# Second attention of a graph-network kernel: exponentials straight from PSUM, a shift from the first columns, one-input looks, a shorter epilogue, the reciprocal root as a power on GpSimd

## Chip, core and metric

One core of one Trainium2 chip. The metric is the device time of one execution in microseconds (us). The repeats of one kernel differ by under 0.4%. In profile lines PE is the engine that multiplies matrices (TensorE), DVE is VectorE, ACT ScalarE and POOL GpSimd; L12 is line 12 of the kernel that was run, so line numbers differ between kernels.

## The reference, cut to what matters

Four graph layers on 3327 nodes with 256 features. The change concerns the last one, which runs two steps of an attention whose rows keep only their largest probabilities, up to 90% of the mass:

```python
for n in range(STEPS):                       # 2 steps; the change is in the second
    q, k = Xa @ W1.T @ W2.T, Xa @ W3.T
    probs = softmax(q @ k.T)                 # 3327 x 3327
    A = probs * (smallest set of largest entries with sum >= 0.9)
    A = A / A.sum(-1)
    Xf = R @ Xf                              # diffusion, R = normalized (adj + I)
    Xa = A @ Xa
    Z = Z + Xf @ U1[n].T + Xa @ U2[n].T
h = layernorm(X + Z) * g + b
return layernorm(X + h)
```

## The kernel before: the parts concerned

Rows are worked in 26 tiles of 128. A tile ("a row" from here on) is searched one ahead: `ahead(it + 1)` makes the logits of the next row and searches them while `step(it)` attends, diffuses and finishes this one. The text is not the order of execution: the framework fixes the order of each engine's instructions at compile time, and the place in the text is only one of the things that decide it.

```python
# logits(): eight pieces of 416 columns, each copied out of PSUM
for c0 in range(0, half, KC):
    for a in (0, DA):
        nc.tensor.matmul(pl[:, :w], q[a:a + DA, :], kT[a:a + DA, c0:c0 + w], start=True, stop=True)
        nc.scalar.copy(e[:, c:c + w], pl[:, :w])

def search_long(work, e, total, v, kept):
    nc.vector.max(m8, e)                               # needs the whole row
    nc.vector.tensor_scalar(hneg, m8[:, 0:1], -0.5, LN15 / 2, ...)
    nc.scalar.activation(junk, e, AF.Exp, bias=hneg, scale=0.5, accum_out=root)
    exponentials(e, m8[:, 0:1], total)                 # e = exp(e - max), total = its sum
    c1 = 0.301 * (total / root) ** 2                   # first threshold
    nc.scalar.activation(junk, e, AF.Sign, bias=c1, scale=-1.0, accum_out=sg)   # count
    over(c1, m1)                                       # "look": mass of e >= c1, two inputs
    ...                                                # c2 by small steps
    over(c2, m2)
    ...                                                # c3
    nc.vector.scalar_tensor_tensor(z, e, c3, e, is_lt, mult, accum_out=rest)
    top = ranked(work, segment_tops(work, z), RPT)     # 32 MAX8 of 104 columns, 7 rounds
    ...
    for k in range(0, TIES, 8):                        # two full-width replaces
        nc.vector.match_replace(z, rep[:, k:k + 8], z if k else e, 2.0)
    nc.vector.scalar_tensor_tensor(e, z, v, e, is_gt, mult, accum_out=kept)   # "last product"

es = [ahead(0)]
for it in range(nt):
    if it + 1 < nt:
        es.append(ahead(it + 1))
    step(it, ...)                                      # attention, diffuse, finish
```

## Time and profile before

| | us |
|---|---|
| time, median of 4 | 5088.1 (5085.5 to 5091.3) |
| one row of the second attention | 54.06 |
| of it DVE works / stands still | 46.4 / 7.7 |
| PE works / ACT works | 40.6 / 23.1 |

A row is the mean distance between the starts of the masking product into `z` in successive rows; work is the busy time of an engine in windows of whole rows, and standstill is the rest. The groups, windows, waits and chain stand in the prediction below. This is the timeline of ACT in one row of the kernel before (start us, us, line, what):

```profile
4726.40 1.28 ACT L70 ACT_TABLE_LOAD   x1
4727.70 0.29 ACT L70 ACTIVATE std<-mv,eps_t 128x1 f32<-128x1 f32 x1
4728.01 1.28 ACT L439 ACT_TABLE_LOAD   x1
4729.31 3.07 ACT L439 ACTIVATE e<-e,neg 128x3328 f32<-128x3328 f32 x1
```

Between the two exponentials of this row ACT loads a table for the root, takes a root of one column, and loads the exponentials' table again, while DVE waits for the second exponential: two loads of 1.28 us. This is the worst place; in the whole stage 7 loads stand in front of the full-scale exponential (L439) as here, and 24 in front of the half-scale one (L474).

### The profile page before, as it was taken

Reading aid. Unit: us, or ns where it says so; the run is one execution under the profiler, and the core shown is the slowest. Engines: PE = TensorE matmul, PEld = TensorE weight load, DVE = VectorE, ACT = ScalarE, POOL = GpSimd, SP = SyncE. Lnnn points to the kernel's source line nnn. Section 1 sums busy time; section 2 is a strip of 40 time slices with the busy share of each in tenths; the row PEclk is TensorE's granted clock in tenths of the full one; section 3 lists DMA queues with packets and bytes.
Section 4 is the critical chain, followed back from the end, with each engine's and each line's share of the span. In section 5 each row is a group of like instructions: output and inputs, shape, how many; then the busy total and the mean of one; then the engine's idle time right before and its main releaser. Section 6 shows DMA issues by size and latency. Waiting matters only on the chain. (4 is left out here: it accounts for less than half of the span.)

```text
span 5089.8 us, 44369 instructions
## 1 busy us (share of the span) xinstructions
PE 4067.5 (80%) x16218; PEld 2926.3 (57%) x16218; DVE 3402.9 (67%) x6846; ACT 1790.1 (35%) x2868; POOL 5.5 (0%) x58
## 2 busy tenths in 40 slices
PE   8999986677767776779978999999577778787686
PEld 7878862222322223567756777777366556565565
DVE  1111129798797988799944544453388888888886
ACT  0001124334343243355533333333333443443442
POOL 0000000000000000000000000000000000000000
PEclk9999987777777777889978999999588888888888
DMA  5433320000000000122211111111001001011010
GB/s 176 137 127 132 131 74 0 0 0 0 0 0 0 0 0 0 58 94 105 102 35 35 47 54 54 50 45 54 1 29 43 30 30 43 29 36 38 30 34 27
DMA packets 59325, 239.76 MB, mean 47 GB/s; under 512 B 7105, under 2 KB 21568, under 8 KB 55632
## 3 DMA queue, kind: packets, MB, share of 16 engines
q1 hardware_dynamic: 59088, 236.74, 14.0%
q8 instruction: 132, 2.16, 0.2%
q14 instruction: 105, 0.86, 0.1%
HBM read 233.31 MB, written 3.41 MB: 47 GB/s over the span
## 5 line engine op out<-in xcount | busy, mean ns | idle before, releaser
L105 PE MATMUL acc<-X,at 128*128 128x256 f32 x2704 | 611.4, 381 | 11.9 <-DMA at<-in_adjT 11.9
L271 PE MATMUL y<-db,ident 128*128 128x512 f32 (+1 forms) x896 | 501.0, 715 | 138.6 <-DVE db L269 138.4
L105 PEld LDWEIGHTS acc<-X,at 128*128 128x128 f32 x2704 | 508.5, 191 | 77.4 <-issue 12.3
L265 DVE TENSOR_TENSOR_SCAN h<-dA,carry,db 128x512 f32<-128x512 f32 (+1 forms) x448 | 504.3, 1188 | 2.2
L253 PE MATMUL ps<-dbc,ident 48*128 48x512 f32 (+1 forms) x448 | 294.1, 783 | 226.6 <-ACT row L256 226.6
L271 PEld LDWEIGHTS y<-db,ident 128*128 128x128 f32 x896 | 207.7, 244 | 453.3 <-DVE db L269 239.4
L118 ACT COPY wt<-ps 128x512 f32<-128x512 f32 (+1 forms) x546 | 278.6, 555 | 448.2 <-PE ps L116 444.4
L116 PE MATMUL ps<-ident,e 128*128 128x128 f32 x1352 | 204.7, 301 | 252.7 <-DVE e L545 215.7
L260 ACT ACTIVATE dA<-dt,A_log 128x512 f32<-128x512 f32 (+1 forms) x448 | 273.0, 680 | 371.8 <-DVE h L265 371.7
L120 PE MATMUL acc<-Xa,wt 128*128 128x256 f32 x1352 | 340.0, 407 | 15.5 <-ACT wt L118 14.5
L116 PEld LDWEIGHTS ps<-ident,e 128*128 128x128 f32 x1352 | 176.6, 156 | 297.5 <-issue 270.2
L120 PE MATMUL acc<-H,wt 128*128 128x256 f32 x1352 | 313.9, 386 | 29.0 <-ACT wt L118 26.4
L120 PE MATMUL acc<-X,wt 128*128 128x256 f32 x1352 | 310.2, 383 | 21.5 <-ACT wt L118 19.3
L253 PEld LDWEIGHTS ps<-dbc,ident 48*128 48x128 f32 x448 | 96.6, 242 | 392.7 <-ACT row L256 276.7
L94 ACT COPY xt<-ps 128x256 f32<-128x256 f32 x234 | 82.5, 374 | 651.9 <-PE ps L92 629.5
L120 PEld LDWEIGHTS acc<-Xa,wt 128*128 128x128 f32 x1352 | 272.7, 206 | 66.8 <-ACT wt L118 27.1
L105 PE MATMUL acc<-xa,at 128*128 128x257 f32 x1352 | 307.4, 381 | 0.0
L105 PE MATMUL acc<-Xf,at 128*128 128x256 f32 x1352 | 301.7, 379 | 0.0
L120 PEld LDWEIGHTS acc<-H,wt 128*128 128x128 f32 x1352 | 251.7, 191 | 76.8 <-ACT wt L118 44.7
L120 PEld LDWEIGHTS acc<-X,wt 128*128 128x128 f32 x1352 | 252.5, 190 | 70.3 <-ACT wt L118 38.2
L415 PE MATMUL ps<-kT,q 64*128 64x416 f32 x832 | 255.0, 615 | 36.8 <-ACT q L401 25.8
L105 PEld LDWEIGHTS acc<-xa,at 128*128 128x128 f32 x1352 | 255.2, 190 | 36.9 <-issue 0.7
(238 smaller groups left out, 6006.4 us busy)
## 6 DMA issues: line engine op xcount, KB each, us to landing
at<-in_adjT SPq DMA_DIRECT2D x104, 832.0 KB, 4.4
at<-in_adjT SPq DMA_DIRECT2D x104, 576.0 KB, 3.7
ad<-in_adj SPq DMA_DIRECT2D x26, 1663.5 KB, 6.8
at<-in_adjT SPq DMA_DIRECT2D x52, 512.0 KB, 3.5
xa<-in_x SPq DMA_DIRECT2D x1, 3328.0 KB, 12.7
xt<-in_xT SPq DMA_DIRECT2D x26, 128.0 KB, 4.0
out<-h SPq DMA_DIRECT2D x25, 128.0 KB, 1.7
w_in<-in_w_in SPq DMA_DIRECT2D x1, 1024.0 KB, 5.1
```

The costliest lines, as they stand in the source:

```text
L94: nc.scalar.copy(t, pt)
L105: nc.tensor.matmul(acc, at[:, j, :], rhs[:, j0 + j, :], start=(j0 + j == 0), stop=(j0 + j == nt - 1))
L116: nc.tensor.transpose(pt[:, j, :], w[:, (j0 + j) * P:(j0 + j + 1) * P], ident)
L118: nc.scalar.copy(wt[:, :m, :], pt[:, :m, :])
L120: nc.tensor.matmul(acc, wt[:, j, :], rhs[:, j0 + j, :], start=(j0 + j == 0), stop=(j0 + j == nt - 1))
L253: nc.tensor.matmul(ps[:, :w], ident[:R, r:r + 1].to_broadcast([R, P]), dbc[:, :w], start=True, stop=True)
L260: nc.scalar.activation(dA[:, g, :], dt[:, g, :], AF.Exp, scale=A[:, g, s:s + 1])
L265: nc.vector.tensor_tensor_scan(h[:, g, :], dA[:, g, :], db[:, g, :], initial=carry[:, s, g:g + 1], op0=ALU.mult, op1=ALU.add)
L271: nc.tensor.matmul(ys[g][:, :w], ident, db[:, g, :], start=(s == 0), stop=(s == DS - 1))
L415: nc.tensor.matmul(pl[:, :w], q[a:a + DA, :], kT[a:a + DA, c0:c0 + w], start=True, stop=True)
```

## The change

Its intent: DVE bounds the second attention, so take a full-width maximum and some small instructions off it, let the exponentials start as soon as pieces of logits arrive, and keep ACT in one table. The exponentials read the logits where PE leaves them (PSUM) instead of a copy. The shift is what is subtracted before the exponential: it was the maximum of the whole row and is now that of its first piece of 416 columns.

```diff
+            q = query(work, psum, xs, it)
+            for i in range(nk):                              # eight pieces
+                nc.tensor.matmul(pl, q[a:a + DA, :], kT[a:a + DA, c0:c0 + w], start=True, stop=True)
+                if neg is None:                              # first piece alone
+                    nc.vector.max(m8, pl)
+                    nc.vector.tensor_scalar_mul(neg, m8[:, 0:1], -1.0)
+                    nc.vector.tensor_scalar_mul(hneg, m8[:, 0:1], -0.5)
+                nc.scalar.activation(e[:, c:c + w], pl, AF.Exp, bias=neg, accum_out=totals[:, i:i + 1])
+                nc.scalar.activation(junk[:, :w], pl, AF.Exp, bias=hneg, scale=0.5, accum_out=roots[:, i:i + 1])
+            nc.vector.reduce_sum(total, totals, axis=AX.X)
+            nc.vector.reduce_sum(root, roots, axis=AX.X)
...
-                nc.vector.scalar_tensor_tensor(djunk, e, c, e, op0=ALU.is_ge, op1=ALU.mult, accum_out=m)
+                nc.vector.tensor_scalar(djunk, e, c, 0.0, op0=ALU.max, op1=ALU.add, accum_out=f)
+                nc.scalar.activation(ajunk, e, AF.Sign, bias=c, scale=-1.0, accum_out=sg)   # in both looks
+                nc.vector.tensor_scalar(k, sg, -0.5, npad / 2, op0=ALU.mult, op1=ALU.add)
+                nc.vector.tensor_scalar(m, k, -float(npad), c, op0=ALU.add, op1=ALU.mult)
+                nc.vector.tensor_add(m, m, f)
...
         def diffuse(...):
-            nc.vector.tensor_add(t, acc, xs[:, it, :])
-            nc.vector.tensor_scalar_mul(dst, t, rdeg[:, it:it + 1])
+            nc.gpsimd.tensor_scalar(t, xs[:, it, :], rdeg[:, it:it + 1], None, op0=ALU.mult)
+            nc.vector.scalar_tensor_tensor(dst, acc, rdeg[:, it:it + 1], t, op0=ALU.mult, op1=ALU.add)
...
         def finish(...):                                     # twice: variance -> rstd
+            nc.gpsimd.tensor_scalar(rs, mv[:, 1:2], EPS, None, op0=ALU.add)
+            nc.gpsimd.tensor_tensor(rs, rs, mhalf, op=ALU.pow)
-            layernorm(h, h)
-            nc.vector.tensor_mul(h, h, g3)
-            nc.vector.tensor_add(h, h, b3)
-            nc.vector.tensor_add(h, h, X[:, it, :])
-            layernorm(h, h)
+            nc.vector.scalar_tensor_tensor(h, h, mv[:, 0:1], g3, op0=ALU.subtract, op1=ALU.mult)
+            nc.vector.scalar_tensor_tensor(h, h, rs, xb, op0=ALU.mult, op1=ALU.add)
+            ...
+            nc.scalar.activation(h, h, AF.Identity, scale=rs, bias=nb)
```

More of the change, by code (lines that the diff above doesn't have):

```diff
@@ L34 @@
 UNDER = 24.0
+HUGE = 1e38
 KC = 416
@@ L365, in gnn_kernel @@
         nc.vector.memset(ones, 1.0)
+        mhalf = pool.tile([P, 1], F32, name="mhalf")
+        nc.vector.memset(mhalf, -0.5)
         count = pool.tile([P, TIES], F32, name="count")
@@ L454, in limit, with search_short @@
             return lim
-        def search_short(work, e, total, v, kept):
+        def search_short(work, psum, xs, kT, it, total, v, kept):
+            e = logits(work, psum, xs, kT, it, 3)
             top = ranked(work, segment_tops(work, e), RP0)
@@ L463, in search_short, with search_long, t1 @@
             nc.vector.scalar_tensor_tensor(e, e, v, e, op0=ALU.is_ge, op1=ALU.mult, accum_out=kept)
-        def search_long(work, e, total, v, kept):
-            m8 = sm.tile([P, 8], F32, name="m8")
-            nc.vector.max(m8, e)
-            hneg = sm.tile([P, 1], F32, name="hneg")
-            nc.vector.tensor_scalar(hneg, m8[:, 0:1], -0.5, LN15 / 2, op0=ALU.mult, op1=ALU.add)
-            junk = work.tile([P, npad], BF16, name="ajunk", bufs=1)
-            root = sm.tile([P, 1], F32, name="root")
-            nc.scalar.activation(junk, e, AF.Exp, bias=hneg, scale=0.5, accum_out=root)
-            exponentials(e, m8[:, 0:1], total)
+            return e
+        def search_long(work, psum, xs, kT, it, total, v, kept):
+            def t1(name, w=1):
+                return sm.tile([P, w], F32, name=name)
+            e = work.tile([P, npad], F32, name="e", bufs=3)
+            if npad > n:
+                nc.gpsimd.memset(e[:, n:], 0.0)
+            q = query(work, psum, xs, it)
+            neg, hneg = None, None
+            nk = half // KC * 2
+            roots, totals = t1("roots", nk), t1("totals", nk)
+            for i in range(nk):
+                a, c0 = (0, DA)[i % 2], i // 2 * KC
+                c = c0 + (half if a else 0)
+                w = min(KC, n - c)
+                pl = psum.tile([P, 512], F32, name="ps")[:, :w]
+                nc.tensor.matmul(pl, q[a:a + DA, :], kT[a:a + DA, c0:c0 + w], start=True, stop=True)
+                if neg is None:
+                    m8 = t1("m8", 8)
+                    nc.vector.max(m8, pl)
+                    neg, hneg = t1("neg"), t1("hneg")
+                    nc.vector.tensor_scalar_mul(neg, m8[:, 0:1], -1.0)
+                    nc.vector.tensor_scalar_mul(hneg, m8[:, 0:1], -0.5)
+                nc.scalar.activation(e[:, c:c + w], pl, AF.Exp, bias=neg, accum_out=totals[:, i:i + 1])
+                junk = work.tile([P, KC], BF16, name="rjunk")
+                nc.scalar.activation(junk[:, :w], pl, AF.Exp, bias=hneg, scale=0.5, accum_out=roots[:, i:i + 1])
+            root = t1("root")
+            nc.vector.reduce_sum(total, totals, axis=AX.X)
+            nc.vector.reduce_sum(root, roots, axis=AX.X)
             lim = limit(total)
-            def t1(name):
-                return sm.tile([P, 1], F32, name=name)
             c1 = t1("c1")
@@ L484, in search_long, with look @@
             nc.vector.scalar_tensor_tensor(c1, c1, 0.301, c1, op0=ALU.mult, op1=ALU.mult)
-            z = work.tile([P, npad], F32, name="z", bufs=1)
-            djunk = work.tile([P, npad], BF16, name="djunk", bufs=1)
-            def over(c, m):
-                nc.vector.scalar_tensor_tensor(djunk, e, c, e, op0=ALU.is_ge, op1=ALU.mult, accum_out=m)
-            m1, m2, sg = t1("m1"), t1("m2"), t1("sg")
-            nc.scalar.activation(junk, e, AF.Sign, bias=c1, scale=-1.0, accum_out=sg)
-            over(c1, m1)
-            rc = t1("rc")
+            def look(c, i):
+                f, sg, k, m = (t1(f"{x}{i}") for x in ("lf", "ls", "lk", "lm"))
+                djunk = work.tile([P, npad], BF16, name="djunk", bufs=1)
+                nc.vector.tensor_scalar(djunk, e, c, 0.0, op0=ALU.max, op1=ALU.add, accum_out=f)
+                ajunk = work.tile([P, npad], BF16, name="ajunk", bufs=1)
+                nc.scalar.activation(ajunk, e, AF.Sign, bias=c, scale=-1.0, accum_out=sg)
+                nc.vector.tensor_scalar(k, sg, -0.5, npad / 2, op0=ALU.mult, op1=ALU.add)
+                nc.vector.tensor_scalar(m, k, -float(npad), c, op0=ALU.add, op1=ALU.mult)
+                nc.vector.tensor_add(m, m, f)
+                return k, m
+            k1, m1 = look(c1, 1)
+            rc, na = t1("rc"), t1("na")
             nc.vector.reciprocal(rc, c1)
-            na, k1 = t1("na"), t1("k1")
             nc.vector.tensor_scalar(na, m1, lim, rc, op0=ALU.subtract, op1=ALU.mult)
-            nc.vector.tensor_scalar(k1, sg, -0.5, npad / 2, op0=ALU.mult, op1=ALU.add)
             den, nu, p, q = t1("den"), t1("nu"), t1("p"), t1("q")
@@ L512, in search_long @@
             nc.vector.tensor_sub(big, k1, na)
-            nc.vector.tensor_scalar(big, big, 32.0, 1e9, op0=ALU.is_lt, op1=ALU.mult)
-            over(c2, m2)
+            nc.vector.tensor_scalar(big, big, 32.0, HUGE, op0=ALU.is_lt, op1=ALU.mult)
+            k2, m2 = look(c2, 2)
             s, dm, lo, hi = t1("s"), t1("dm"), t1("lo"), t1("hi")
@@ L530, in search_long @@
             rest, base = t1("rest"), t1("base")
+            z = work.tile([P, npad], F32, name="z", bufs=1)
             nc.vector.scalar_tensor_tensor(z, e, c3, e, op0=ALU.is_lt, op1=ALU.mult, accum_out=rest)
@@ L535, in search_long @@
             cs = crossing(work, v, top, 8 * RPT, base, lim)
-            r, rep = t1("r"), sm.tile([P, TIES], F32, name="rep")
+            r, rep = t1("r"), t1("rep", TIES)
             nc.vector.tensor_sub(cs, cs, top)
@@ L540, in search_long @@
             nc.vector.scalar_tensor_tensor(cs, cs, lim, top, op0=ALU.is_lt, op1=ALU.mult, accum_out=r)
-            nc.vector.tensor_scalar(rep, count, r, -5.0, op0=ALU.is_ge, op1=ALU.mult)
+            nc.vector.tensor_scalar(rep, count, r, -HUGE, op0=ALU.is_ge, op1=ALU.mult)
             nc.vector.tensor_scalar_add(rep, rep, v)
             for k in range(0, TIES, 8):
-                nc.vector.match_replace(z, rep[:, k:k + 8], z if k else e, 2.0)
+                nc.vector.match_replace(z, rep[:, k:k + 8], z if k else e, HUGE)
             nc.vector.scalar_tensor_tensor(e, z, v, e, op0=ALU.is_gt, op1=ALU.mult, accum_out=kept)
+            return e
         def normalizer(kept, total):
@@ L619, in diffuse, with rstd @@
         def diffuse(work, atp, psum, dst, xs, it):
+            t = work.tile([P, D], F32, name="t")
+            nc.gpsimd.tensor_scalar(t, xs[:, it, :], rdeg[:, it:it + 1], None, op0=ALU.mult)
             acc = aggregate(atp, psum, it, xs, D, 9)
-            t = work.tile([P, D], F32, name="t")
-            nc.vector.tensor_add(t, acc, xs[:, it, :])
-            nc.vector.tensor_scalar_mul(dst, t, rdeg[:, it:it + 1])
+            nc.vector.scalar_tensor_tensor(dst, acc, rdeg[:, it:it + 1], t, op0=ALU.mult, op1=ALU.add)
+        def rstd(mv):
+            rs = sm.tile([P, 1], F32, name="rs3")
+            nc.gpsimd.tensor_scalar(rs, mv[:, 1:2], EPS, None, op0=ALU.add)
+            nc.gpsimd.tensor_tensor(rs, rs, mhalf, op=ALU.pow)
+            return rs
         def finish(work, psum, it, xf2, xa2):
+            xb = work.tile([P, D], F32, name="t")
+            nc.gpsimd.tensor_tensor(xb, X[:, it, :], b3, op=ALU.add)
             pz = psum.tile([P, D], F32, name="acc")
@@ L632, in finish @@
             nc.vector.tensor_add(h, pz, X[:, it, :])
-            layernorm(h, h)
-            nc.vector.tensor_mul(h, h, g3)
-            nc.vector.tensor_add(h, h, b3)
-            nc.vector.tensor_add(h, h, X[:, it, :])
-            layernorm(h, h)
+            mv = sm.tile([P, 2], F32, name="mv3")
+            stats(mv, h)
+            rs = rstd(mv)
+            nc.vector.scalar_tensor_tensor(h, h, mv[:, 0:1], g3, op0=ALU.subtract, op1=ALU.mult)
+            nc.vector.scalar_tensor_tensor(h, h, rs, xb, op0=ALU.mult, op1=ALU.add)
+            mv = sm.tile([P, 2], F32, name="mv3")
+            stats(mv, h)
+            rs = rstd(mv)
+            nb = sm.tile([P, 1], F32, name="nb")
+            nc.vector.scalar_tensor_tensor(nb, mv[:, 0:1], -1.0, rs, op0=ALU.mult, op1=ALU.mult)
+            nc.scalar.activation(h, h, AF.Identity, scale=rs, bias=nb)
             m = min(P, n - it * P)
@@ L674, in ahead @@
                 def ahead(it):
-                    e = logits(work, psum, xs, kT, it, 3)
-                    search(work, e, tot_all[:, it:it + 1], v_all[:, it:it + 1], kept_all[:, it:it + 1])
-                    return e
+                    return search(work, psum, xs, kT, it, tot_all[:, it:it + 1], v_all[:, it:it + 1], kept_all[:, it:it + 1])
                 es = [ahead(0)]
```

## The prediction

> **What bounds the kernel now**
>
> I read the page first (slices, costliest groups), then a table of windows over the last third, then the groups by form, the waits and the chain inside the second attention only. The slices show PE at 9 tenths nearly everywhere up to slice 28 and dropping to 5 to 8 after it, while DVE rises to 8: the last eleven or twelve slices are the second attention, and there the bound changes hands. It runs from about 3637 us (where DVE starts on its first row) to the end at 5089.8, so some 1453 us or 29% of the span. Almost all of the change lies in it; in the first attention only the small diffusion epilogue changes.
>
> Its 26 row tiles repeat in a pattern of three (three e buffers). The windows of three such patterns, columns as in their head line:
>
> ```profile
> core 0: us, PE busy (x) PEld busy (x) DVE busy (x) ACT busy (x) POOL busy (x), PEclk, DMA share, GB/s
> 3200.00:3300.00 100.00, 93.87 (x456) 75.04 (x455) 48.84 (x183) 35.37 (x66) 0.29 (x3) 1.00 0.16 52
> 4149.50:4312.25 162.75, 122.07 (x536) 97.31 (x535) 139.15 (x369) 69.19 (x101) 0.29 (x3) 0.85 0.11 34
> 4312.25:4473.90 161.65, 121.30 (x536) 96.11 (x535) 139.04 (x369) 69.28 (x101) 0.29 (x3) 0.86 0.11 35
> 4473.90:4636.60 162.70, 122.05 (x536) 97.24 (x535) 139.19 (x369) 69.18 (x101) 0.29 (x3) 0.85 0.11 34
> ```
>
> A row thus takes (162.75+161.65+162.70)/9 = 54.1 us; DVE works 46.4 of it (86%), PE 40.6, ACT 23.1. The first line is the first attention: there PE works 94% at clock 1.00. So in the second attention PE is not the limit; it waits, and its clock falls to 0.85. DVE stands still 7.7 us a row. What it waits for, over the whole stage:
>
> ```profile
> DVE lim L453 <- ACT e L439: 84.9, 25, 3.9
> DVE c L482 <- ACT ajunk L474: 56.8, 17, 4.5
> DVE t L622 <- PE acc L105: 26.7, 5, 23.9
> DVE h L632 <- PE acc L630: 16.0, 14, 3.5
> DVE rs L71 <- ACT std L70: 13.4, 11, 2.2
> ```
>
> The reader is to see that the two exponentials of a row cost DVE (84.9+56.8)/26 = 5.4 us of standstill a row, though ACT is not full: they cannot start before the row's maximum is known, and the maximum needs the whole copied row. The chain inside three rows says the same: DVE lines for the most part, and the two exponentials in between.
>
> ```profile
> by line: DVE djunk L489 13.7%; DVE z L544 11.9%; DVE cand L423 10.0%; issue 8.2%; DVE z L531 6.9%; DVE m L469 6.5%; ACT e L439 5.8%; DVE top L430 4.5%; DVE cand L432 4.1%; ACT ajunk L474 3.0%; DVE e L545 2.4%; PE acc L630 2.1%; ACT L474 1.6
> ```
>
> Durations that I use (last numbers before the bar are the mean ns of one):
>
> ```profile
> L489 DVE SCALAR_TENSOR_TENSOR djunk<-e,c 128x3328 bf16<-128x3328 f32 x52 | 191.6, 3684 | 1.8
> L469 DVE MAX8 m<-e 128x8 f32<-128x3328 f32 x26 | 93.7, 3602 | 72.1 <-ACT e L416 72.1
> L79 DVE TENSOR_SCALAR h<-h,mv,rs 128x256 f32<-128x256 f32 x52 | 21.3, 410 | 0.5
> L635 DVE TENSOR_TENSOR h<-h,ln_b 128x256 f32<-128x256 f32 x26 | 10.9, 419 | 0.1
> L623 DVE TENSOR_SCALAR xf<-t,rdeg 128x256 f32<-128x256 f32 x26 | 8.7, 335 | 0.0
> L498 DVE TENSOR_SCALAR na<-m,lim,rc 128x1 f32<-128x1 f32 x26 | 7.1, 272 | 0.0
> L439 ACT ACTIVATE e<-e,neg 128x3328 f32<-128x3328 f32 x26 | 79.8, 3069 | 0.4
> L474 ACT ACT_TABLE_LOAD x24 | 30.8, 1283 | 65.8 <-DVE hneg L471 55.9 <-DVE neg L438 9.7
> ```
>
> **What the Trainium skill says**
>
> "VectorE: DVE Perf Modes", section "The perf-mode tier table", gives an fp32 SBUF tensor_scalar two elements a cycle and a tensor_tensor one. The trace agrees: the standardize of 256 columns takes 410 ns where the same form on one column takes 272, so 138 ns for the columns, half of the 267 that the second form's 419 contains. That would make a one-input look of 3328 columns some 1.75 us shorter than the two-input one. But "SBUF — State Buffer", section "Who interferes with whom", excepts from the two-port modes the form of tensor_scalar that also writes out its accumulator, and the looks are that form. No instruction of the kernel before is of that form, so its trace cannot decide. I follow the page: no gain in rate.
>
> "ScalarE: Activation LUTs", section "What ACT_TABLE_LOAD costs", gives 1283 ns for a load (the trace: 1283) and about 280 ns + 0.833 ns a column for an activation with a pointer bias (3052 for 3328 columns; the trace: 3069). For 416 columns that is an estimate of 0.63 us. Its section "Table sets" puts exp and sqrt in different sets, which is why the trace has 63 loads in this stage (32 at the square root, 24 and 7 at the exponentials).
>
> "GPSIMD Engine Reference", section "Elementwise — side-by-side cycle accounting", has GpSimd about half as fast as DVE on two inputs; a 128x256 add would then be an estimated 0.8 us. GpSimd is empty here (under 0.1 us a row), so only its latency can matter. No trace shows a power there.
>
> **The change part by part, per row of the second attention**
>
> 1. *Row maximum.* Out: one MAX8 over 3328 columns, 3.60. In: one over 416 columns from PSUM; the slope is 3602/3328 = 1.08 ns, so about 0.55 with overhead. DVE -3.05.
> 2. *Looks.* Two two-input looks of 3.68 plus a 0.08 read become two one-input looks of, by the page, about 3.6 plus 0.08: -0.1 (at the double rate it would be -3.6). Each now needs a Sign count on ACT (the first had it). More small steps on the path: k, m, m for each look in place of one k in all, about +0.85, and two short sums of partial totals, +0.35.
> 3. *Epilogue.* Diffusion: 0.42+0.33 becomes one 0.42: -0.33. Finish: out are two reciprocals (0.31), two standardizes (0.82), three tensor_tensors (1.26); in are two scalar_tensor_tensors (0.84) and one small product (0.15): -1.4. Both also take 63 table loads (1.28 each, 3.1 us a row) off ACT.
>
> Sum on DVE: -3.05-0.1+0.85+0.35-0.33-1.4 = -3.7, so 46.4 becomes 42.7 us of work a row.
>
> 4. *Exponentials from PSUM.* Out on ACT: eight copies (about 0.43 to 0.5 each, 3.7), two exponentials and their reads (6.4), the loads (3.1), two roots (0.6): -13.8. In: 16 exponentials of 416 columns, each with an accumulator read. In the trace an exponential with its read advances ACT by 3.19 us for 3328 columns; 2912 columns less at 0.833 leave 0.76, so 16 x 0.76 = 12.2; a second Sign (3.2); a last scaling of 128x256 (0.47). +15.9. ACT goes from 23.1 to about 25 us a row, still half of the row.
>
> What matters more is when they run. The exponentials no longer wait for a complete row; they can run while DVE ranks and replaces in the row before (about 20 us of DVE work), so most of the 5.4 us standstill should go. But not all: the first maximum and its two sign changes stand somewhere in DVE's strict order behind a 3.6 us instruction or two, then 12.2 us of ACT follow, and the first constant of the search waits for the last sum. I leave 3.5 us of the 7.7 of standstill.
>
> Row: 42.7 + 3.5 = 46.2 us against 54.1, -7.9. Times 26: -205. Filling and draining change little: the first row saves a maximum and part of its two exponentials (about 5 us), the last finish perhaps 1. The first attention loses 0.33 us of DVE a row where DVE is half idle and PE works 94%: nothing.
>
> 5090 - 205 - 5 = 4880; I put it at 4890, since a schedule seldom gives all.
>
> **Rivals**
>
> *PE and ACT take over in the logits.* Today PE makes a row's eight pairs of logits in 4.5 us; each bank will now be held for two exponentials, 1.5 us, so the stage lasts 12.2 and PE, with three such banks, is held by ACT for 7 to 8 us. If PE ran attention (16.5), diffusion (11.2), finish (5.5), query (2) and logits (12.5) strictly in this order after each search, a row would be 47.7 us plus handing over, about 48.5, whatever DVE saves: -146, a time of 4945. For it: this is PE's order in two of the three rows of the pattern, and PE is in order. Against it: in the third row the diffusion's matmuls are already interleaved with the attention's, so the static order does fill PE's gaps with the next ready work. Denser work would also lift PE's clock from 0.86 towards the 1.00 of the first attention.
>
> *The looks run at the double rate.* Then DVE falls to 39 us, PE (40.6 busy, about 37 to 39 at clock 1.00) and DVE are level, and a row is 43 to 45: 4805 to 4855. For it: plain tensor_scalars do so in this trace. Against it: the page's exception.
>
> *Only the work goes and the standstill stays.* The wait for the exponentials moves from the long ones to the last of sixteen short ones, or the second Sign is late for the second look because ACT is at attention's copies. Then -3.7 x 26 = -96: 4994, within 2%.
>
> *GpSimd's small steps stretch the finish.* A variance goes DVE, GpSimd twice, DVE, twice a row. If each trip cost 2 us of standstill, 4 us a row would be lost. The roots' trips cost DVE 13.4/26 = 0.5 us a row before, with table loads, because other DVE work was put between; I expect the same.
>
> **Range and chances**
>
> The 8-in-10 range covers the double-rate looks at half their effect on one side (4825) and a PE and ACT bound row with some handing over on the other (4970). Faster by over 2% means under 4988, 3.9 us a row; the work removed from DVE alone is 3.7, so almost any gain of overlap suffices: 0.87. Within 2%: 0.11, if the standstill stays or a new one comes. Slower: 0.02, for an order in which PE, ACT and DVE wait for one another in turn.
>
> **What would show it right or wrong**
>
> Right: no full-width maximum and no table loads in the rows; looks of 3.6 to 3.7 us; DVE busy near 42.7 us a row and over 90% of it; the wait for the exponentials under 2 us a row; ACT near 25. A look near 2 us means the page's exception doesn't hold here. The PE bound shows as matmuls of the logits waiting for the exponentials by 5 us or more a row with DVE under 88%. A long wait of the normalizing steps for GpSimd shows the last rival. All this fails as a whole if rows before the last third change their length, or if the fallback search for unresolved rows runs, which would show as a new stretch of work after a pass.

## The result, and the profile after

| | before | after |
|---|---|---|
| time, median of 4 | 5088.1 | 5079.1 (5077.4 to 5079.8) |
| ratio after to before | | 0.9981, 95% interval 0.9964 to 0.9999 |
| one row of the second attention | 54.06 | 54.06 |
| DVE works / stands still, a row | 46.4 / 7.7 | 43.9 / 10.2 |
| ACT works, a row | 23.1 | 22.3 |

Ratios are the mean time of one kernel's fast runs over that of the other's in the same rounds, so not quite the ratio of the medians quoted. 4890 was predicted, within 4825 to 4970: wrong. The row did not get shorter at all. What was gained is from before the steady rows: in the profiled executions the third row's masking product starts at 3755.57 us against 3770.30, and from there on rows of both kernels take 54.0 to 54.1 us (at the end these two executions are 13.2 us apart, the medians 9.0).

A window of three rows of the changed kernel (columns as in its head line):

```profile
core 0: us, PE busy (x) PEld busy (x) DVE busy (x) ACT busy (x) POOL busy (x), PEclk, DMA share, GB/s
4314.24:4476.40 162.16, 126.25 (x537) 93.56 (x536) 131.61 (x376) 66.95 (x157) 9.91 (x21) 0.84 0.11 35
```

DVE's work fell from about 139 us in three rows to 131.61 (131.70 and 131.66 in the windows beside it), but the window of three rows is as long as before. What fills it is in the waits (us in total, times, longest):

```profile
PE ps L492 <- ACT rjunk L501: 248.3, 48, 10.1
ACT e L499 <- DVE neg L497: 240.3, 24, 10.5
DVE tot_all L503 <- ACT e L499: 186.6, 24, 8.9
```

The wait for the totals, 186.6/24 = 7.8 us a row, has taken the place of the two waits for exponentials, 5.4 us a row. And there is a line that the kernel before did not have in this size: ACT itself waits 240.3/24 = 10.0 us a row for `neg`, the sign-changed first-columns maximum, which DVE makes. So DVE waits for ACT in each row, after ACT has waited for DVE. One row of DVE's timeline shows both (start us, us, line, what, and in brackets idle time before it):

```profile
4588.62 3.61 DVE L573 MATCH_REPLACE8 z<-rep,z 128x3328 f32<-128x3328 f32 x1
...
4592.48 3.67 DVE L574 SCALAR_TENSOR_TENSOR e<-z,v_all,e 128x3328 f32<-128x3328 f32 x1
...
4596.17 0.56 DVE L495 MAX8 m<-ps 128x8 f32<-128x416 f32 x1
...
4599.40 0.16 DVE L681 SCALAR_TENSOR_TENSOR nb<-mv,rs 128x1 f32<-128x1 f32 x1 [0.86 <-POOL rs L659]
4607.28 0.16 DVE L503 TENSOR_REDUCE tot_all<-totals 128x1 f32<-128x8 f32 x1 [7.72 <-ACT e L499]
```

PE and ACT in the same stretch:

```profile
4598.56 1.75 PE L492 MATMUL ps<-kT,q 64*128 64x416 f32 x2 [10.06 <-ACT rjunk L501]
```

```profile
4597.22 0.61 ACT L499 ACTIVATE e<-ps,neg 128x416 f32<-128x416 f32 x1 [10.44 <-DVE neg L497]
```

PE has made three pieces of logits since 4586.83 and then waits 10.06 us for a free bank. ACT waits 10.44. Both wait for a MAX8 of 0.56 us whose operand has long been there: it stands in DVE's order behind both full-width replaces (L573, which start at 4584.70 and 4588.62) and the last product (L574) of the row before, and starts at 4596.17. Only then do sixteen exponentials begin, with the last scaling of the finish between them, and DVE, which has no full-width work left, stands still from 4599.56 to 4607.28. "Idle" in DVE's bracket names ACT, but the delay was made by DVE's own order, which let the MAX8 start only 11.1 us before.

The MAX8 stands like this behind the last product in all rows but the first two, which start before any last product. So DVE did not take it earlier although its operand was there; runs x2, x8 and x10 below change this place.

The chain of three rows has the exponentials in it now, and no full-width maximum:

```profile
by line: DVE djunk L515 13.6%; DVE z L573 13.4%; DVE cand L426 10.0%; ACT rjunk L501 7.6%; DVE z L560 6.9%; DVE e L574 6.6%; ACT e L499 6.5%; DVE cand L435 5.5%; DVE top L433 5.5%; issue 2.2%; POOL t L664 1.3%; ACT h L682 1.1%; POOL rs L659
```

Three of the groups that the prediction had sized (the last number before the bar is the mean ns of one):

```profile
L515 DVE TENSOR_SCALAR_CACHE_REDUCE djunk<-e,c 128x3328 bf16<-128x3328 f32 x52 | 191.3, 3679 | 2.1 <-DVE c L509 0.4
...
L501 ACT ACTIVATE rjunk<-ps,hneg 128x416 bf16<-128x416 f32 x182 | 112.5, 618 | 0.0
L499 ACT ACTIVATE e<-ps,neg 128x416 f32<-128x416 f32 x182 | 112.2, 617 | 243.0 <-DVE neg L497 243.0
```

### The profile page after: what moved, and what is told of

Read it like the earlier page. It is cut to its first block, busy times and chain, and to the rows that moved or that the text cites. A ratio compares the mean times of both kernels' runs of the same rounds, so it can differ in the third digit from the quotient of the medians.

```text
span 5076.6 us, 45120 instructions
## 1 busy us (share of the span) xinstructions
PE 4122.1 (81%) x16218; PEld 2917.9 (57%) x16218; DVE 3328.7 (66%) x6873; ACT 1779.1 (35%) x3351; POOL 113.7 (2%) x240
## 5 line engine op out<-in xcount | busy, mean ns | idle before, releaser
L492 PE MATMUL ps<-kT,q 64*128 64x416 f32 (+1 forms) x416 | 227.1, 826 | 258.3 <-ACT rjunk L501 249.1
L121 PE MATMUL acc<-Xa,wt 128*128 128x256 f32 x1352 | 323.2, 395 | 2.4 <-ACT wt L119 2.0
L492 PEld LDWEIGHTS ps<-kT,q 64*128 64x128 f32 x416 | 83.3, 266 | 374.8 <-ACT rjunk L501 351.4
L106 PEld LDWEIGHTS acc<-Xf,at 128*128 128x128 f32 x1352 | 255.0, 190 | 33.7
```

The costliest lines, as they stand in the source:

```text
L106: nc.tensor.matmul(acc, at[:, j, :], rhs[:, j0 + j, :], start=(j0 + j == 0), stop=(j0 + j == nt - 1))
L121: nc.tensor.matmul(acc, wt[:, j, :], rhs[:, j0 + j, :], start=(j0 + j == 0), stop=(j0 + j == nt - 1))
L492: nc.tensor.matmul(pl, q[a:a + DA, :], kT[a:a + DA, c0:c0 + w], start=True, stop=True)
```

## The experiments

Theory A, formed from that profile: a row is set by a serial loop. DVE's order holds the first-columns maximum back until the row before is done; then 9.4 us of exponentials run on ACT; then DVE goes on. The work taken off DVE shortens nothing, because the exponentials cannot begin until the work of the row before is over and now stand in series with it: DVE lost 2.5 us of work a row and gained 2.5 of standstill. Rival B: ACT's many short exponentials, or the detour over GpSimd, are the limit wherever they start.

### x1: no maximum

```diff
-                    m8 = t1("m8", 8)
-                    nc.vector.max(m8, pl)
-                    neg, hneg = ...
+                    neg, hneg = shift[:, 0:1], shift[:, 1:2]     # constants -20 and -10
```

> The changed kernel with a fixed shift of 20 in place of the first columns' maximum, so that the exponentials wait for no DVE instruction; the results stay right for these inputs. Theory A (the exponentials start late because the maximum of the first 416 columns stands in DVE's order behind the row before's last full-width instruction, at 4596.2 us in one row though its logits were there at 4587.3, and then 9.4 us of exponentials run while DVE stands still): the standstill before the sum of the totals falls from 7.8 us a row to under 2, a row from 54.06 to 45 to 47 us, the time from 5079 to 4840 to 4900. Rival B (ACT's sixteen exponentials and sixteen accumulator reads a row are the limit wherever they start, or the GpSimd detour in the finish is): under 50 us gained.

4914.1 us, ratio 0.9658; results correct. The row is 47.06 us. The wait for the totals fell to 12.8 us in the whole stage. The gain of 165 us against the changed kernel clears rival B; it is 14 us short of the range that I gave. (The run also drops the MAX8 and its two products, 0.57 and 0.15 twice, so at most 0.9 us a row of the 7.0 is work; x2 keeps them.)

### x2: the maximum moved within DVE's order

The search is cut in two in the text, so that the start of the next row (query, logits, maximum, exponentials) is written ahead of the second replace, and an order-only dependence holds the second replace behind `hneg`. Same instructions, same results.

```diff
+            nc.vector.match_replace(z, rep[:, 0:8], e, HUGE)
+            def rest_of(after):                       # called after start_long(it + 2)
+                ins = nc.vector.match_replace(z, rep[:, 8:16], z, HUGE)
+                tc.add_manual_dep(ins.ins, after.ins.name, NoSync)    # after = hneg of row it + 2
+                nc.vector.scalar_tensor_tensor(e, z, v, e, op0=ALU.is_gt, op1=ALU.mult, accum_out=kept)
```

> The changed kernel with only the order of DVE changed: the next row's first-columns maximum and its two products stand between the two full-width replaces of the row before instead of after them and after the full-width product. Same instructions, same results. Theory A: the exponentials start some 7.5 us earlier in each row, the standstill of 7.8 us shrinks to 1 to 2, a row takes 46 to 48 us, the time is 4860 to 4920. Rival B: 5030 to 5080, because the wait only changes its name.

4927.2 us, ratio 0.9683: 152 us under the changed kernel, by order alone, 7 us outside my range. The row is 47.58 us and the wait for the totals 9.6 us in the stage. In both kernels' timelines PE goes through a row in the same sequence (finish, query, logits, attention, diffusion), so it is DVE's order that was moved.

### x3: the half-scale exponentials twice

```diff
+                nc.scalar.activation(junk[:, :w], pl, AF.Exp, bias=hneg, scale=0.5, accum_out=roots[:, i:i + 1])
```

> The changed kernel with each of the eight half-scale exponentials of a row issued twice; same results. ACT's busy time rises from 22.3 to some 27 of 54 us a row. Theory A (every exponential lies in series with DVE's standstill): eight more of 0.587 us are 4.7 us a row, times 26 = 122, so about 5200 us. Rival C (ACT is 41% busy, its slack takes them): under 30 us more.

5210.7 us, ratio 1.024: 132 us more than the changed kernel, 122 expected. The row is 59.3 us. Both sums are waited for longer:

```profile
DVE tot_all L504 <- ACT e L499: 248.9, 22, 12.4
DVE root L505 <- ACT rjunk L502: 38.4, 21, 1.8
```

(248.9+38.4)/22 = 13.1 us a row against 7.9 in the changed kernel (7.8 for the totals and 4.0/24 = 0.2 for the roots): 5.1 more, as much as the row grew. ACT was busy 41% of the time, yet had no slack that counts: the added exponentials lay in series with DVE.

### The parts alone: x4, x6, x7

x4 is the kernel before with the new `diffuse` and `finish`; x6 is it with the one-input looks alone; x7 with the exponentials from PSUM alone (square roots stay). Each edit is the corresponding part of the diff above.

> The kernel before with only the new epilogue: one fused step in the diffusion, two fused steps in the finish, the power on GpSimd in place of square root and reciprocal, the last scaling on ACT. Theory A: DVE loses some 1.5 us of work a row (39 us in all) and the exponentials' wait loses the table loads that lie in it, some 0.9 us a row (22), so 5020 to 5040 us. Rival D (the detour over GpSimd costs what the fused steps save): 5080 to 5100.

> The kernel before with only the one-input looks. Theory A: 0.7 to 1.1 us a row more, 5106 to 5120 us. Rival: at or under 5088, because ACT's counts are hidden and the small steps are too.

> The kernel before with only the exponentials from PSUM and the shift from the first columns; square roots, and so the table loads, stay. Theory A: DVE loses 2.7 us of work a row, but the maximum comes to stand behind the row before's last instruction in every row, 9.4 us of exponentials and one or two table loads of 1.28 us run while DVE stands still, so the standstill grows by more than the work shrinks: 5090 to 5160 us. Rival E (the exponentials alone would gain, and the loss comes from one of the other parts): under 5060.

| alone | time | against its own rounds' before |
|---|---|---|
| x4 epilogue | 5011.1 | -76.7, ratio 0.9849 |
| x6 one-input looks | 5113.5 | +27.8, ratio 1.0053 |
| x7 exponentials from PSUM | 5127.1 | +41.4, ratio 1.0081 |
| sum of the three | | -7.5 |
| the whole change | 5079.1 | -9.0, ratio 0.9981 |

So the whole is nearly nothing: one gain meets two losses, and the three add up to it within 2 us. The epilogue gave more than expected (5020 to 5040), the other two lie within what was expected. In x7 the roots that stayed now fall among the sixteen exponentials; its groups of table loads, in 23 rows:

```profile
L71 ACT ACT_TABLE_LOAD x46 | 59.0, 1283 | 0.8
...
L499 ACT ACT_TABLE_LOAD x24 | 30.8, 1283 | 0.4
L501 ACT ACT_TABLE_LOAD x22 | 28.2, 1283 | 0.4
```

Four loads a row, where the kernel before has 63 in 26 rows. The 1.6 loads more are 2.0 us a row, as much as the row of x7 is longer (55.99 us), so x7 alone doesn't show that the exponentials themselves lost. x4 and x5 (below) do: neither has a load in these rows, x5 is x4 with the exponentials from PSUM, and it takes 49 us more (5060.4 against 5011.1).

### x9: the power alone

x4 gave 77 us. Its row is 50.69 us, DVE works 89.6% of it, 45.4, against 46.4 before; so the work fell by 1.0 and the standstill by 2.5. To see which of its parts did that:

```diff
-            layernorm(h, h)               # standard deviation by ACT's square root, then reciprocal
+            layernorm3(h)                 # the same, rstd by GpSimd's add and power; no step fused
```

> The kernel before with only the power on GpSimd in place of square root and reciprocal in the finish; no step fused. The whole epilogue gave 77 us while DVE's work fell by only 1.1 us a row and its standstill by 2.5. Theory A: nearly all of that standstill was table loads that lay in front of the exponentials and broken order around the square roots; so the power alone gives 50 to 70 us: 5018 to 5038. Rival F (the fused steps are what counted): 5068 or more.

5027.4 us, ratio 0.988: 61.5 of the 77 us, within what was expected. The row is 51.39 us, DVE works 89.8% of it, 46.2: its work fell by only 0.2 (the two reciprocals are gone), and nearly the whole gain is standstill. DVE's waits of x9 for the two exponentials (21 to 22 rows):

```profile
DVE lim L455 <- ACT e L441: 64.2, 21, 3.9
...
DVE c L484 <- ACT ajunk L476: 8.7, 3, 3.2
```

The wait for the half-scale exponential has shrunk from 56.8/26 = 2.2 us a row to 8.7/21 = 0.4: no table has to be loaded in front of it. The reciprocal root on GpSimd costs DVE about 1 us a row of waiting (22.1 us in the same rows), less than the square roots had cost with their loads. What the loads cost and what the roots themselves cost, x9 doesn't separate.

### x5 and x8: two-input looks in the changed order and in the moved one

```diff
-            k2, m2 = look(c2, 2)          # one input, and a count on ACT
+            over(c2, m2)                  # two inputs, no count; likewise c1, with the count of before
```

> The changed kernel with the looks undone: two-input looks as before, a count by ACT in the first alone. In the changed kernel a one-input look takes 3679 ns against 3684 before, so it has no rate of its own to give; what it brings is a second count on ACT and some 0.85 us a row of small steps on DVE's path. Theory A: 0.7 to 1.1 us a row less, 5045 to 5062 us. If the one-input form helps in a way that the durations don't show: 5079 or more.

> The kernel of the moved maximum (4927 us) with the looks undone as well: exponentials from PSUM, new epilogue, two-input looks. There DVE works 93% of the time, so its work sets the row. Theory A: 0.7 to 1.1 us a row less, 4898 to 4910 us, the fastest so far. If PE (90% in that kernel) has become the limit: 4920 to 4930.

x5 (the changed kernel with this edit): 5060.4 us, ratio 0.995, as expected. It is also epilogue and exponentials together, 25 us under the kernel before, where x4 and x7 alone sum to 35 under it: these two add less exactly than all three did. x8 (x2 with this edit): 4878.7 us, ratio 0.9595, better than expected and 4% under both kernels. Its window over fifteen rows (columns as in the window above):

```profile
4118.70:4798.90 680.20, 631.67 (x2672) 477.19 (x2673) 646.28 (x1801) 288.11 (x752) 101.14 (x104) 0.88 0.14 41
```

DVE works 95%. A part of one row of it:

```profile
4322.59 0.58 DVE L495 MAX8 m<-ps 128x8 f32<-128x416 f32 x1
...
4323.80 3.61 DVE L580 MATCH_REPLACE8 z<-rep,z 128x3328 f32<-128x3328 f32 x1
...
4333.11 0.15 DVE L512 TENSOR_REDUCE tot_all<-totals 128x1 f32<-128x8 f32 x1
```

The MAX8 now stands between the replaces, at 4322.59; 3.6 + 3.7 us of DVE work cover the exponentials, and the sum of the totals starts with no bracket for ACT; in the whole stage it waits once, 1.5 us. (Just before it DVE waits 0.78 us for the power on GpSimd, which hides a wait for ACT up to that length.) Undoing the looks saved 19 us in the first order and 48 in the second. The small steps fit the first (a row of 53.24 against 54.06, and small steps of 0.88); of the 2.2 us a row in the second, its work is 1.0 (44.1 against 43.1, from 92.7% of 47.58 and 95.0% of 45.38), and the rest is standstill. The waits show where: in 20 rows of x2 DVE waits 9.8 us for the first piece of logits, 9.1 for the two sums and 4.0 for the finish's product, about 1.1 us a row; in 21 rows of x8 it waits 3.2 us for the logits and nothing for the others. Why undoing the looks removes these waits wasn't followed further.

### x10: the maximum one instruction later

```diff
-            nc.vector.match_replace(z, rep[:, 0:8], e, HUGE)
+            for k in range(0, TIES, 8):
+                nc.vector.match_replace(z, rep[:, k:k + 8], z if k else e, HUGE)
             def rest_of(after):                       # called after start_long(it + 2)
-                ins = nc.vector.match_replace(z, rep[:, 8:16], z, HUGE)
+                ins = nc.vector.scalar_tensor_tensor(e, z, v, e, op0=ALU.is_gt, op1=ALU.mult, accum_out=kept)
                 tc.add_manual_dep(ins.ins, after.ins.name, NoSync)
-                nc.vector.scalar_tensor_tensor(e, z, v, e, op0=ALU.is_gt, op1=ALU.mult, accum_out=kept)
```

Against x8.

> The kernel of 4879 us with the maximum one full-width instruction later in DVE's order: behind both replaces, in front of the last product. Between it and the kernel with the maximum behind the last product (5060 us) there is one full-width instruction of 3.7 us a row. Theory A (the place in the order alone sets when the exponentials start): 3.7 x 26 = 96 us under 5060, 4950 to 4980. Rival: at 5060 or at 4879, if something else starts the exponentials.

4967.2 us (one of four runs 4949.7), ratio 0.975. Its wait for the totals (us, times, longest):

```profile
DVE tot_all L512 <- ACT e L499: 80.6, 22, 4.9
```

That is 80.6/22 = 3.7 us a row, between 7.8 in the changed kernel and next to nothing in x8. With the maximum behind the last product, in front of it, and in front of the second replace as well, a row takes 53.24, 49.29 and 45.38 us: about one full-width instruction (3.7 and 3.6 us) less each time. The place in DVE's order sets the row here, as theory A has it.

### x11: copies instead of exponentials from PSUM, with the order seen to

The kernel before with the new epilogue (x4) and the whole row's maximum pinned in front of the last product.

> The kernel before with the new epilogue and the whole row's maximum pinned in front of the last full-width product of the row before; logits are still copied and the exponentials run over the whole row. It asks what exponentials from PSUM give against a copy when both have their order seen to. Theory A: DVE keeps the 3.6 us maximum, but no standstill of more than 2 us a row is left: 4910 to 4960, so the exponentials from PSUM are worth 30 to 80 us in the right order. If the order was no trouble in the kernel before: 5011, as without the pin.

A miss: 5023.4 us, ratio 0.9875, no better than x4 without the pin.

The pin took hold (in one row the maximum starts at 4307.17, the last product at 4310.93), but the product's 3.7 us cover only part of the two long exponentials: in the waits of x11, 51.8/21 = 2.5 us a row still go to the full-scale one, and the 3.6 us maximum is still DVE's (90.3% of a row of 51.17, 46.2). I had left 2 us of standstill in all; it is 5.0. With the maximum at the same place, in front of the last product, exponentials from PSUM and the shift from the first columns are worth 5023.4 (x11) to 4967.2 (x10), 56 us. Against the best kernel with copies (x4, 5011.1) the best with exponentials from PSUM (x8, 4878.7) is 132 us ahead, but copies with the maximum in front of the second replace as well, as in x8, were not tried, so these 132 are not a like-for-like comparison. The part that lost 41 us alone is in the fastest kernel.

### x12: the last small product on GpSimd

```diff
-            nc.vector.scalar_tensor_tensor(nb, mv[:, 0:1], -1.0, rs, op0=ALU.mult, op1=ALU.mult)
+            nc.gpsimd.tensor_scalar(nb, mv[:, 0:1], rs, -1.0, op0=ALU.mult, op1=ALU.mult)
```

> The kernel of 4879 us with the last small product of the finish on GpSimd in place of DVE, which stands still 0.75 us a row for the power in front of it and needs 0.16 for the product itself. If DVE still sets the row: 0.5 to 0.9 us a row less, 4855 to 4866. If PE (93% of the time there) sets it: 4872 to 4882.

4880.5 us, ratio 0.959: no different from x8. The wait of 0.75 us a row is gone and the row is 45.34 us all the same, so little of it was on the path. Part of it only hid another: behind it DVE now waits 0.17 us a row for the last half-scale exponential (4.0 us, 24 times; once, 0.2 us, in x8). PE is at 93% there, but that PE sets this row isn't shown.

## Why the prediction was wrong, point by point

- *The slices and the start of the stage.* Misread, without effect on the sums: PE stands at 9 tenths in only 12 of the first 28 slices (6 to 8 in the others), and DVE's first row starts at 3644 us, not 3637.
- *DVE bounds the second attention (86% busy), PE doesn't.* Right as a reading of busy time; but of the 8.7 us a row that x8 saves, 5.4 come out of the standstill, and the share of busy time said nothing of how that would move.
- *Work leaving DVE: -3.7 us a row.* Measured -2.5. By term: the maximum 3602 to 569 ns, -3.03 (-3.05 predicted). Looks 3684 to 3679 ns, no gain in rate, as the SBUF page's exception has it. Small steps of the looks +0.88 and sums +0.32, by their durations (+0.85 and +0.35). Diffusion 415+335 to 475 ns, -0.28; finish -1.28, because the fused steps take 469 and 485 ns, not 420. By durations -3.4, of which only 2.5 show as busy time. Durations overlap and busy time counts an overlap once; in windows of 21 rows all of DVE's durations together fell from 52.9 to 49.7 us a row, so the overlaps shrank by 0.7. The last 0.2 is not settled.
- *ACT goes to about 25 us.* 22.3. The term "16 x 0.76 = 12.2" was mis-sized: an exponential and its accumulator read of 416 columns advance ACT by 0.587 us, so 9.4 in all. My 0.76 came from a 3328-column exponential in the trace of before, whose fixed part did not carry over to short ones in a row. This error made the prediction too slow, not too fast.
- *"They can run while DVE ranks and replaces in the row before ... I leave 3.5 us of the 7.7 of standstill."* This is the step that failed. The standstill rose to 10.2. I had seen that the first maximum would stand in DVE's strict order "behind a 3.6 us instruction or two"; it stands behind the last full-width instruction of the row, in every row but the first two, so nothing was left for the exponentials to hide behind. x10 and x8 against x5 show that this place alone is worth 3.9 us a row for each full-width instruction, x2 that order alone takes 6.5 us off the row, and x3 that exponentials added there lie in series. Of the 7.9 us by which the row was mispredicted (54.06 against 46.2) this step is 6.7 (10.2 against 3.5), and the work of the point above 1.2 (43.9 against 42.7).
- *Rival "PE and ACT take over in the logits".* Its picture came true in part, PE held 10 us at the third piece, and DVE was under 88% (81%), which is the sign that the prediction had named for it; but the holder was the maximum, not ACT's pace. x1 took the maximum away and the row fell to 47, and x8's 45.4 is under the 48.5 that this rival held for a floor. Its side remark that denser work lifts PE's clock didn't come out: PE 75% busy at 0.86 before, 79% at 0.82 in the changed kernel, 93% at 0.88 in x8.
- *Rival "only the work goes and the standstill stays", 4994.* Nearest to what happened, and still too good, because the standstill grew by as much as the work fell. I gave 0.11 to a time within 2%.
- *"GpSimd's small steps stretch the finish".* Not to the 4 us feared: DVE's wait for the power is 22.4/26 = 0.9 us a row, against the 0.5 expected.
- *"The roots' trips cost DVE 13.4/26 = 0.5 us a row".* Too narrow a reading: that wait was small, but table loads that come with the roots stood in front of the exponentials, where DVE waited under another name. x9 shows that taking roots and loads off ACT is worth 61.5 us, with 0.2 us a row of work leaving DVE.
- *The row of 46.2 us* is not out of reach: the same instructions in another order (x2) take 47.6, and with the looks undone as well (x8) 45.4. That x8's 4878.7 us is near the 4890 predicted is no confirmation: it is another kernel, without the looks.

## What to carry to other kernels

When an instruction is moved to make a chain start earlier, find its place in the list of the engine that executes it: a half-microsecond instruction that feeds a long chain on another engine, placed behind that engine's long work, can undo the move, and the wait is then shown under the other engine's name. Take work off an engine only after asking which of its waits starts the next round; here 3.3 of the 8.7 us a row that the best version saves were work, and the rest was standstill, mostly from order and from the roots with their table loads. When a change of several parts gives nothing, run the parts alone, and the losing part again with its order seen to: it may be the best one.

## What the Trainium skill lacked or had wrong

- "VectorE: DVE Perf Modes", section "The perf-mode tier table": its row gives fp32 tensor_scalar the double rate without exception. With an accumulator output it took 3679 ns for 3328 columns, the single rate. "SBUF — State Buffer", section "Who interferes with whom", names the exception, and the run agrees with it.
- "ScalarE: Activation LUTs", section "What ACT_TABLE_LOAD costs": 1283 ns for a load holds, but the page adds a drain and makes it 2.66 us for a switch. In the timeline shown above a load starts at 4726.40 and the root behind it at 4727.70: 1.30 us. The estimate of 0.63 us for a 416-column activation, worked out from the page's figures, holds (617 ns); it has no figure for the accumulator read, here about 0.19 to 0.29 us, a pair of the two advancing ACT by 0.587 us.
- "GPSIMD Engine Reference": section "Engine selection" calls one-input work roughly line rate; here a one-input 128x256 multiplication by a column took 942 ns and a two-input 128x256 addition 722 ns (0.8 estimated), both in the changed kernel and as rough as POOL's spans are. The addition doesn't keep its time: in x8, where it starts just behind DVE's 3.7 us last product (4327.88 against 4327.72 us in one row), it takes 4.10 us. No page gives a power: 567 ns on 128x1.
- No page that I used says how an ordering made at compile time can place a short instruction behind long ones; here that place was worth 182 us (5060.4 to 4878.7).
